# Layer 1's sum over neighbours of 24 batches computed in the second pass, beside the LSTM, and kept in DRAM

## The chip, the cores and the metric

The kernel runs on one core of a Trainium2 chip. The metric is the device time of one execution in microseconds (us). A core has five engines that run side by side, each with its own in-order queue of instructions: TensorE (PE; the loading of its weights is listed apart as PEld), VectorE (DVE), ScalarE (ACT), GpSimd (POOL) and SyncE (SP), which here issues nearly all of the DMAs.

## The reference

The input is x, 32 batches of 512 nodes with 128 features, and adj, a symmetric 0/1 matrix of 512x512 for each batch with ones on its diagonal. Four layers are applied, each to the ReLU of a normalised x, and each result is added to x. Layer 0 is attention masked by adj. Layer 1 is the one that the change touches:

```python
def preprocess_adj(A):
    A_hat = A + jnp.eye(N, dtype=A.dtype)
    d = jnp.sum(A_hat, axis=2)
    ...
    return d_inv[:, :, None] * A_hat * d_inv[:, None, :]      # d_inv = d ** -0.5

def gcn_dynamic_forward(x, A_norm, conv_w, conv_b, w_ih, w_hh, b_ih, b_hh):
    df_in = x[:, x.shape[1] - HID:, :]                         # the last 128 nodes
    dyn = jax.lax.conv_general_dilated(df_in, conv_w, ...) + conv_b[None, :, None]
    lw = lstm(dyn, w_ih, w_hh, b_ih, b_hh)                     # 128 steps, all batches at once
    agg = jnp.matmul(A_norm, x)
    return jax.nn.sigmoid(jnp.matmul(agg, lw))
```

The LSTM needs only the last 128 nodes of layer 0's result, and its output lw is needed only in the last product. So agg, the sum over neighbours, does not depend on the LSTM. Layer 2 has four message-passing steps, each with a sum over neighbours by the normalised matrix, and layer 3 one more.

## The kernel before

The kernel doesn't write its instructions down in their final order. It records operations with their engine, an estimated duration, a rank (lower is more urgent) and the tiles that they read and write; a planner, `Plan.run`, then plays them through with these durations and fixes each engine's order. A tile has a tag, and `BUFS` says how many buffers a tag has; an operation whose tile has no free buffer has to wait. On the chip each engine works through its list in that order, and an instruction that waits holds up all that is behind it on its queue.

There are three stages.

- **`pass_1(b)`** for all 32 batches: normalise x, project keys, queries and values, and compute attention for the last 128 nodes only, then the convolution. It keeps keys and hidden rows (`f_dkq`), values (`f_dv`) and the last 128 rows of x (`f_dl`) in DRAM.
- **`lstm()`** with **`pass_2(b)`** beside it. The 128 LSTM steps are urgent (rank below 1000). A step is: 16 small matmuls on PE (`f_z`, L1193), a tanh on ACT (L1219, and L1234 for the fourth gate), three operations on DVE that make the cell state (L1226 to L1228), a tanh on ACT (L1236), and two operations on DVE that write the hidden state (L1240, L1241); the next step's matmuls wait for it. Between them the planner puts `pass_2`, the attention of the other 384 nodes: load `f_kq`, three quarters of the rows of the matrix (`f_a`, 768 KB), `f_v` and x; then `f_pq` (L1259), four products `f_s` (L1268), exponentials and masks (L1271, L1272), twelve products `f_po` (L1277), the update of x (L1283) and its store `f_dx` (L1285), mean and variance (L1008, L1010), and the reciprocal root on POOL. `fold(i)` prepares layer 2's weights in the same stage. A filler that would run past the expected start of an urgent operation by more than 0.05 us is held back.
- **`rest(b)`**, the third stage, after the LSTM: load the whole matrix (1024 KB) and x, square the matrix on ACT (L1329; its accumulated rows are the degrees), make the degree factors on POOL (`norms`, L1335), normalise x with them (`ln_apply`), split the ReLU into two parts of a shorter number format (`relu_parts`, L1303 and L1304), add the identity to the matrix on DVE (L1356), sum over neighbours on PE (`aggregate`, L1313, eight matmuls of 128x512 into `f_pg`), take the identity off again, evict the sum (`f_gT`), and multiply it by the LSTM's output (`gates`, L1372). Then come layers 2 and 3. The matrix also goes to DRAM as bfloat16 (`f_das`, L1387, issued by POOL), comes back transposed (`f_aT`, L1389), and DVE compares the two (`f_junk`, L1392); if some matrix were not symmetric, a general kernel would run instead.

The batches of a stage overlap. The last two batches' `pass_2` is planned among the first batches of the third stage, and the first batches of `rest` begin before the LSTM has ended.

Of the kernel before, what the change touches and what calls it, by code (L numbers as in the profile page):

```python
# [520 lines left out]
class Plan:  # L521
# [19 lines left out]
    def __init__(self, bufs, fifo, banks):  # L541
        self.banks = banks
        self.last = float("inf")
        self.spared = float("inf")
        self.left = 0
        self.sealed = 0
        self.ops = []
        self.bufs = bufs
        self.made = {}
        self.fifo = {t: [] for t in fifo}  # L550
# [40 lines left out]
    def run(self, tc, queues):  # L591
# [63 lines left out]
        def room(o):  # L655

            at = 0.0
            need = {}
            for c in o.cells:
                if c not in seen:  # L660
                    if c.tag in self.fifo and self.fifo[c.tag][turn[c.tag] + need.get(c.tag, 0)] is not c:
                        return None
                    need[c.tag] = need.get(c.tag, 0) + 1
            for t, n in need.items():
                if len(slots[t]) < n + (t == self.banks and o.rank >= self.spared and self.left > 0):
                    return None
                at = max(at, sorted(slots[t])[n - 1])
            return at
# [4 lines left out]
        done, order = 0, []  # L673
        while done < len(ops):
            best = None
            for e, cands in pools.items():
                first = None
                held = expected.get(e)
                for rank, no, o in cands:
                    r = room(o)  # L680
                    if r is None:
                        continue
                    if r:
                        r += self.HOP
                    s = max(free[e], o.ready[e], r)
                    if len(o.engines) > 1:
                        mine = s + o.engines[e][0]
                        if any(max(free[x], o.ready[x], r) + o.engines[x][0] < mine - 1e-9 for x in o.engines if x != e):
                            continue
                    if rank < self.URGENT:  # L690
                        held = s
                    elif held is not None and s < held < s + o.engines[e][0] - 0.05:
                        continue
                    if first is None or s < first[0] - 1e-9:
                        first = (s, o)
                        if s <= free[e] + 1e-9:
                            break
                if first is not None and (best is None or first[0] < best[0]):
                    best = (first[0], e, first[1])
# [25 lines left out]
            order.append(o)  # L725
            done += 1
# [7 lines left out]
def symmetric(ctx, tc, x, adj, weights, cols, rows, lstm_b, prelu_a, out, fail):  # L734
# [19 lines left out]
    LATE = 2  # L754
    FOLDS = (4, 7, 10, 13)
    MOVED = range(2, B - 2)
    TURN = 32
    T_STEP, T_SWITCH = 0.26, 0.1
    assert D == P and N == 512

    BUFS = {"a": 2, "ar": 6, "x": 7, "xn": 5, "y": 5, "gs": 5, "inv": 4, "n0": 4, "n1": 4, "n2": 4, "n3": 4, "low": 3, "hp": 2, "dt": 2, "mm": 8, "st": 4, "mv": 4, "rs": 4, "sh": 4, "dg": 4, "dv": 4,
# [23 lines left out]
    def new(tag, shape, name, dtype=FP):  # L785
        return plan.cell(sb, tag, shape, dtype, name)
# [22 lines left out]
    def PE(rank, t, fn, r=(), w=(), **k):  # L809
        return plan.op({"PE": (t, fn)}, rank, r, w, **k)  # L810
# [209 lines left out]
    def ln_apply(rank, xc, mean, rstd, shift, r, name, relu=False):  # L1020

        xn = new("xn", (P, NT, P), f"f_xn_{name}")
# [224 lines left out]
    def pass_2(b):  # L1247
        R = 20_000 + b * 10 if b < B - LATE else 30_000 + (b - B + LATE) * 10 + 15
        dkq, dv, dl, dx = kept[b]
        a = new("ar", (P, NT, NR), f"f_a_{b}")  # L1250
        kq = new("y", (P, N + NR), f"f_kq2_{b}")
        v = new("n3", (P, NT, P + 1), f"f_v2_{b}")
        xc = new("x", (P, L, P), f"f_x2_{b}")
        DMA(R, 448, lambda: nc.sync.dma_start(kq.t, dkq.t), [dkq], [kq])
        DMA(R, 768, lambda: nc.sync.dma_start(a.t, adj[b, :, :NR].rearrange("(t p) j -> p t j", p=P)), [], [a])
        DMA(R, 258, lambda: nc.sync.dma_start(v.t, dv.t), [dv], [v])
        DMA(R, 192, lambda: nc.sync.dma_start(xc.t, x[b, :NR].rearrange("(t p) d -> p t d", p=P)), [], [xc])
        pq = bank(f"f_pq_{b}", (P, NR), whole=False)
        PE(R, t_mm(NR), lambda: nc.tensor.matmul(pq.t, w[:, W_Q, :], kq.t[:, N:], start=True, stop=True), [kq], [pq])  # L1259
# [6 lines left out]
        for j in range(NT):  # L1266
            s = bank(f"f_s_{b}_{j}", (P, NR), whole=False)
            PE(R, t_mm(NR), lambda s=s, j=j: nc.tensor.matmul(s.t, kq.t[:, bass.ts(j, P)], q.t, start=True, stop=True),  # L1268
               [kq, q], [s])
            e = new(f"n{j}" if j < 3 else "gs", (P, NR), f"f_e_{b}_{j}")  # L1270
            ACT(R, t_act(NR), lambda s=s, e=e: nc.scalar.activation(e.t, s.t, AF.Exp), [s], [e])  # L1271
            DVE(R, t_dve(NR), lambda e=e, j=j: nc.vector.tensor_mul(e.t, e.t, a.t[:, j, :]), [a], [e])  # L1272
            es.append(e)
# [11 lines left out]
        DMA(R + 5, 192, lambda: nc.sync.dma_start(dx.t, xc.t), [xc], [dx])  # L1285
# [3 lines left out]
        ln_rstd(R, mv, 0, L, (lambda: ln1[:, b, 1, :L], (l1, "rr")))  # L1289

# [17 lines left out]
    def aggregate(rank, parts, ar, pg):  # L1308

        for k in range(2):  # L1310
# [7 lines left out]
    def rest(b, lw_after):  # L1318
# [3 lines left out]
        ar = new("ar", (P, NT, N), f"f_ar_{b}", FR)  # L1322
# [4 lines left out]
        deg = new("dg", (P, NT), f"f_deg_{b}")  # L1327
        for t in range(NT):
            ACT(R, 0.62, lambda t=t: nc.scalar.activation(ar.t[:, t, :], a.t[:, t, :], AF.Square,  # L1329
                                                          accum_out=deg.t[:, t : t + 1]), [a], [(ar, t), (deg, t)])  # L1330
        dinv = new("dv", (P, TURN // NT, NT), f"f_dinv_{b}")
        l1 = lns[b]
        rs = new("rs", (P, NT), f"f_rs_c{b}")

        def norms():  # L1335
# [6 lines left out]
            nc.gpsimd.tensor_mul(rs.t, ln1[:, b, 1, :], d[:, 0, :])  # L1342
        POOL(R, 3.4, norms, [deg, l1], [dinv, rs])
        sh = new("sh", (P, NT), f"f_sh_c{b}")
        ln_shift(R, lambda: ln1[:, b, 0, :], rs, sh, [l1])
        xs = ln_apply(R, xc, lambda t: ln1[:, b, 0, t : t + 1], lambda t: rs.t[:, t : t + 1], lambda t: sh.t[:, t : t + 1],
                      [l1, rs, sh], f"c{b}")
        xp = relu_parts(R, xs, f"c{b}")
# [3 lines left out]
        pg = bank(f"f_pg_{b}")  # L1352

        def diagonal(op):
            blocks = flat(ar.t).rearrange("p (k c) -> p k c", c=P)[:, :: NT + 1, :]
            nc.vector.tensor_tensor(blocks, f32(blocks), ident.unsqueeze(1).to_broadcast([P, NT, P]), op)  # L1356

        DVE(R, t_dve(N), lambda: diagonal(OP.add), [], [ar])

        first = aggregate(R, xp, ar, pg)  # L1360
        DVE(R, t_dve(N), lambda: diagonal(OP.subtract), [], [ar])
        gT = new("gs", (P, N), f"f_gT_{b}")
        evict(R, N, lambda: gT.t, lambda: pg.t, [pg], [gT])
        plw = bank(f"f_plw_{b}", (P, P), whole=False)
        PE(R, T_TR, lambda: nc.tensor.transpose(plw.t, seq[:, :, b], ident), [], [plw], after=lw_after + [first])
# [94 lines left out]
        g3 = new("gs", (P, N), f"f_gT3_{b}")  # L1460
# [144 lines left out]
```

## Time and profile before

| | |
|---|---|
| median of 5 runs | 1339.12 us (1336.26 to 1342.03) |
| the profiled execution | 1338.86 us |
| its span, first to last instruction | 1337.1 us, granted TensorE clock 0.985 |
| busy share of the span | PE 96%, PEld 74%, DVE 76%, ACT 58%, POOL 27% |
| first LSTM matmul, last LSTM matmul group | 186.4 us, 498.5 us |
| moved by DMA | 215.99 MB, mean 162 GB/s |

The groups that the text speaks of (line, engine, operation, out<-in, shape, count, then busy us and mean ns of one, then the idle time of the engine before them):

```profile
L1313 PE MATMUL f_pg<-f_ar,f_xp_c 128*128 128x512 f32 x256 | 74.6, 417 | 4.2 <-ACT f_xp_c L1303 4.2
L1329 ACT ACTIVATE f_ar<-f_a 128x512 fp32r<-128x512 f32 x128 | 78.9, 621 | 3.5 <-PE f_pg L1313 2.1
L1028 ACT ACTIVATE f_xn_c<-f_x,f_sh_c,f_rs_c 128x128 f32<-128x128 f32 x199 | 86.7, 495 | 7.8 <-DVE f_sh_c L1036 7.6
```

Matmuls are pipelined and the ends of their spans are modelled, so the 417 ns of one are not its cost: the distance to the next start is.

### The profile page before, as it was taken

The numbers are of one execution on the slowest core, as the hardware profiler recorded it, in microseconds if no ns is written. First come the engines' busy times: TensorE is split into PE (matmuls) and PEld (weight loads), VectorE is DVE, ScalarE is ACT, GpSimd is POOL, SyncE is SP. The second block draws the span as 40 slices with busy tenths as digits, with TensorE's granted clock in tenths as the row PEclk, the third lists the DMA queues.
The fourth block names the chain that finished last, engine by engine and source line by source line (L and its number), as shares of the span: only waits on it lengthen the run. The fifth ranks groups of instructions, "written<-read, shape, count | busy, mean of one in ns | idle before, by whom it ended". The sixth has DMA issues, their size and how long they took to land. (4 is left out here: it accounts for less than half of the span.)

```text
span 1337.1 us, 26043 instructions
## 1 busy us (share of the span) xinstructions
PE 1286.6 (96%) x8830; PEld 993.4 (74%) x8830; DVE 1012.4 (76%) x3416; ACT 779.9 (58%) x1921; POOL 366.0 (27%) x689
## 2 busy tenths in 40 slices
PE   8999999999999938999999999999999999999996
PEld 6888877776666716787887887787787787787774
DVE  7888867777787848568787787787787787787645
ACT  5566645555556536556666666666666666665433
POOL 4654421111112213222332232232242232232101
PEclk9999999999999968999999999999999999999998
DMA  7879898976676366345566666566666566684211
GB/s 236 283 248 289 264 304 276 285 254 211 189 234 187 84 123 127 86 102 138 130 134 140 134 135 139 135 135 140 133 135 136 141 134 138 139 162 84 48 32 35
DMA packets 287199, 215.99 MB, mean 162 GB/s; under 512 B 136656, under 2 KB 249552, under 8 KB 287056
## 3 DMA queue, kind: packets, MB, share of 16 engines
q1 hardware_dynamic: 270160, 197.45, 54.0%
q0 software_dynamic: 16896, 16.78, 8.0%
q8 instruction: 72, 1.18, 0.4%
q14 instruction: 71, 0.58, 0.2%
HBM read 125.97 MB, written 56.75 MB: 137 GB/s over the span
## 5 line engine op out<-in xcount | busy, mean ns | idle before, releaser
L1313 PE MATMUL f_pa<-f_ar,f_y 128*128 128x512 f32 x1024 | 305.2, 430 | 0.0
L1313 PEld LDWEIGHTS f_pa<-f_ar,f_y 128*128 128x128 f32 x1024 | 189.1, 188 | 74.3 <-issue 41.4
L1419 PE MATMUL f_py<-f_wf,f_n 128*128 128x128 f32 x1280 | 173.9, 275 | 0.0
L1434 ACT ACTIVATE f_n<-f_pa,f_bcol 128x512 f32<-128x512 f32 x128 | 88.4, 691 | 144.0 <-PE f_pa L1430 143.9
L1419 PEld LDWEIGHTS f_py<-f_wf,f_n 128*128 128x128 f32 x1280 | 165.0, 192 | 9.1 <-issue 1.4
L1430 PE MATMUL f_pa<-f_n,f_wf 128*128 128x512 f32 x320 | 152.6, 592 | 0.0
L1387 POOL DMA_DIRECT2D f_das<-f_ar x32 | 37.0, 1155 | 371.5 <-DVE f_ar L1356 364.2
L1295 ACT CAST f_y<-f_py 128x512 fp32r<-128x512 f32 x128 | 74.5, 582 | 74.2 <-PE f_py L1419 50.0
L1277 PEld LDWEIGHTS f_po<-f_v,f_e 128*128 128x128 f32 x768 | 97.3, 191 | 22.8 <-issue 11.9
L1277 PE MATMUL f_po<-f_v,f_e 128*128 128x129 f32 x768 | 109.8, 283 | 0.0
L1193 PE MATMUL f_z<-f_w,f_seq 128*32 128x128 f32 x2040 | 84.1, 283 | 22.6 <-DVE f_seq L1241 16.9
L1426 DVE TENSOR_TENSOR f_pa<-f_pa,f_inv 128x512 f32<-128x512 f32 x128 | 88.3, 692 | 20.1 <-PE f_pa L1313 20.1
L1268 PE MATMUL f_s<-f_q,f_kq 128*128 128x384 f32 x256 | 101.2, 505 | 0.0
L1296 DVE TENSOR_TENSOR f_y<-f_py,f_y 128x512 fp32r<-128x512 f32 x128 | 86.9, 680 | 16.1 <-ACT f_y L1295 16.1
L1193 PEld LDWEIGHTS f_z<-f_w,f_seq 128*32 128x32 f32 x2040 | 49.3, 110 | 61.1 <-issue 15.7
L1392 DVE SCALAR_TENSOR_TENSOR f_junk<-f_a,f_aT 128x1024 bf16<-128x1024 f32 x64 | 78.2, 1222 | 19.6 <-DMA f_aT<-f_das 18.4
L1430 PEld LDWEIGHTS f_pa<-f_n,f_wf 128*128 128x128 f32 x320 | 57.8, 190 | 46.5 <-issue 38.1
L1028 ACT ACTIVATE f_xn_c<-f_x,f_sh_c,f_rs_c 128x128 f32<-128x128 f32 x199 | 86.7, 495 | 7.8 <-DVE f_sh_c L1036 7.6
L1329 ACT ACTIVATE f_ar<-f_a 128x512 fp32r<-128x512 f32 x128 | 78.9, 621 | 3.5 <-PE f_pg L1313 2.1
L840 DVE COPY f_gT<-f_pg 128x512 f32<-128x512 f32 x28 | 19.4, 691 | 79.9 <-PE f_pg L1313 79.8
L1313 PE MATMUL f_pg<-f_ar,f_xp_c 128*128 128x512 f32 x256 | 74.6, 417 | 4.2 <-ACT f_xp_c L1303 4.2
L1219 ACT ACTIVATE f_th<-f_z 128x96 f32<-128x96 f32 x128 | 32.0, 250 | 77.2 <-PE f_z L1193 75.4
(193 smaller groups left out, 2775.6 us busy)
## 6 DMA issues: line engine op xcount, KB each, us to landing
f_a<-in_adj_dram SPq DMA_DIRECT2D x32, 1024.0 KB
f_a<-in_adj_dram SPq DMA_DIRECT2D x32, 768.0 KB
f_das<-f_ar POOLq DMA_DIRECT2D x32, 512.0 KB, 5.1
f_dkq<-f_kh SPq DMA_DIRECT2D x32, 448.0 KB
f_kq<-f_dkq SPq DMA_DIRECT2D x32, 448.0 KB
f_dv<-f_v SPq DMA_DIRECT2D x32, 258.0 KB
f_v<-f_dv SPq DMA_DIRECT2D x32, 258.0 KB
f_x<-in_x_dram SPq DMA_DIRECT2D x32, 256.0 KB
```

The source lines that it names most:

```text
L1028: nc.scalar.activation(xn.t[:, t, :], xc.t[:, t, :], AF.Relu, bias=shift(t), scale=rstd(t))
L1193: nc.tensor.matmul(z.t[part, k, :, :], h, w[:, m : m + 4, part], start=False, stop=True, skip_group_check=True)
L1268: PE(R, t_mm(NR), lambda s=s, j=j: nc.tensor.matmul(s.t, kq.t[:, bass.ts(j, P)], q.t, start=True, stop=True), [kq, q], [s])
L1277: PE(R, t_mm(P), lambda t=t, j=j: nc.tensor.matmul(po.t[:, t, :], es[j].t[:, bass.ts(t, P)], v.t[:, j, :], start=(j == 0), stop=(j == NT - ...
L1296: DVE(rank, t_dve(N), lambda: nc.vector.tensor_sub(parts.t[:, :, 1, :], src.t, f32(parts.t[:, :, 0, :])), [src, (parts, 0)], [(parts, 1)])
L1313: nc.tensor.matmul(pg.t, parts.t[:, j, k, :], ar.t[:, j, :], start=(k == 0 and j == 0), stop=(k == 1 and j == NT - 1))
L1329: ACT(R, 0.62, lambda t=t: nc.scalar.activation(ar.t[:, t, :], a.t[:, t, :], AF.Square, accum_out=deg.t[:, t : t + 1]), [a], [(ar, t), (de ...
L1392: nc.vector.scalar_tensor_tensor(junk, flat(a.t[:, 2 * k : 2 * k + 2, :]), 1.0, flat(aT.t[:, 2 * k : 2 * k + 2, :]), OP.mult, OP.not_equal ...
L1419: nc.tensor.matmul(py.t[:, j, :], nodes[n].t[:, bass.ts(j, P)], wf[:, W_F[i] + c, 0, :], start=False, stop=(c == nch - 1), skip_group_chec ...
L1426: before = DVE(R, t_dve(N), lambda pa=pa: nc.vector.tensor_mul(pa.t, pa.t, inv_row.t), [inv_row], [pa])
L1430: nc.tensor.matmul(pa.t, wf[:, W_F[i] + c, 1, :], nodes[n].t, start=False, stop=(c == nch - 1), skip_group_check=True)
L1434: ACT(R, 0.57, lambda pa=pa, n=n, i=i: nc.scalar.activation(n.t, pa.t, AF.Tanh, bias=bcol[:, i : i + 1]), [pa], [n])
```

## The change

For the batches 0 to 23 (`EARLY`), `pass_2` now also computes layer 1's sum over neighbours. It loads the whole matrix into a buffer of tag `a` and squares it on ACT into tag `ar`; the attention's mask is read from that. It loads the last 128 rows of x too. After the reciprocal root it makes the degree factor on POOL, normalises x in place, splits it, adds the identity to the matrix (on POOL for these batches), sums over neighbours with eight matmuls that are now eight separate operations for the planner, evicts the sum into the tile of x, and stores it in DRAM (`f_dgT`, 256 KB). `rest` loads it from there (`f_gT3`) and has no identity to add and to take off for these batches; it still squares the matrix and makes the degree factors. The batches 24 to 31 are computed as before.

For all batches, keys and hidden rows are loaded as two tiles instead of one, and some tags and counts of buffers change. In the planner, a filler may now run past the expected start of an urgent operation by 0.15 us instead of 0.05, the LSTM step's matmuls are planned with 0.24 us instead of 0.26, and the last free bank of PSUM isn't given to an operation that is ranked far behind the most urgent one left.

```diff
@@ Plan.run @@
+                if len(slots[t]) == n and t in self.kept and by_rank and o.rank > by_rank[-1].rank + 12:
+                    return None
...
-                    elif held is not None and s < held < s + o.engines[e][0] - 0.05:
+                    elif held is not None and s < held < s + o.engines[e][0] - 0.15:
@@ symmetric @@
+    EARLY = range(24)
-    T_STEP, T_SWITCH = 0.26, 0.1
+    T_STEP, T_SWITCH = 0.24, 0.1
...
@@ pass_2 @@
-        a = new("ar", (P, NT, NR), f"f_a_{b}")
-        kq = new("y", (P, N + NR), f"f_kq2_{b}")
+        early = b in EARLY
+        a = new("a" if early else "ar", (P, NT, N if early else NR), f"f_a_{b}")
+        keys = new("inv", (P, N), f"f_k2_{b}")
+        hT = new("xn", (P, NR), f"f_h2_{b}")
...
+        if early:
+            DMA(R, 1024, lambda: nc.sync.dma_start(a.t, adj[b].rearrange("(t p) j -> p t j", p=P)), [], [a])
+            ar, deg = squares(R, b, a, "2")
+            mask, rows_of = ar, lambda j: f32(ar.t[:, j, :NR])
...
+        if early:
+            d = new("dg", (P, NT), f"f_d2_{b}")
+
+            def root():
+                nc.gpsimd.tensor_scalar_add(d.t, deg.t, 1.0)
+                nc.gpsimd.tensor_tensor(d.t, d.t, neg_half[:, 0, :], OP.pow)
+            POOL(R, 1.3, root, [deg], [d])
+            rs = new("rs", (P, NT), f"f_rs_2{b}")
+            POOL(R, 0.34, lambda: nc.gpsimd.tensor_mul(rs.t, ln1[:, b, 1, :], d.t), [d, l1], [rs])
+            gT, _ = sums_of_1(R, b, xc, ar, rs)
+            dg = plan.fixed(dram.tile([P, N], FP, tag=f"g{b}", name=f"f_dgT_{b}"))
+            DMA(R + 5, 256, lambda: nc.sync.dma_start(dg.t, flat(gT.t)), [gT], [dg])
+            kept_sums[b] = dg
+    def diagonal(rank, ar, op, either=False):
+        def on(engine):
+            def fn():
+                blocks = flat(ar.t).rearrange("p (k c) -> p k c", c=P)[:, :: NT + 1, :]
+                engine.tensor_tensor(blocks, f32(blocks), ident.unsqueeze(1).to_broadcast([P, NT, P]), op)
+            return fn
+        if either:
+            POOL(rank, 1.4, on(nc.gpsimd), [], [ar])
+        else:
+            DVE(rank, t_dve(N), on(nc.vector), [], [ar])
+    def sums_of_1(rank, b, xc, ar, rs):
+        l1 = lns[b]
+        sh = new("sh", (P, NT), f"f_sh_c{b}")
+        ln_shift(rank, lambda: ln1[:, b, 0, :], rs, sh, [l1])
+        xs = ln_apply(rank, xc, lambda t: ln1[:, b, 0, t : t + 1], lambda t: rs.t[:, t : t + 1], lambda t: sh.t[:, t : t + 1],
+                      [l1, rs, sh], f"c{b}", place=xc if b in EARLY else None)
+        xp = relu_parts(rank, xs, f"c{b}")
+        pg = bank(f"f_pg_{b}")
+        diagonal(rank, ar, OP.add, b in EARLY)
+        first = aggregate(rank, xp, ar, pg, b in EARLY)
+        gT = xc if b in EARLY else new("gs", (P, N), f"f_gT_{b}")
+        evict(rank, N, lambda: gT.t if b not in EARLY else flat(gT.t), lambda: pg.t, [pg], [gT])
+        return gT, first
@@ rest @@
+        if b in EARLY:
+            gT, first = new("inv", (P, N), f"f_gT3_{b}"), None
+            DMA(R, 256, lambda: nc.sync.dma_start(gT.t, kept_sums[b].t), [kept_sums[b]], [gT])
+        else:
+            gT, first = sums_of_1(R, b, xc, ar, rs)
+            diagonal(R, ar, OP.subtract)
```

## The prediction

> **What bounds the kernel now.** First the windows, one stage to a line (stretch in us: its length, busy us of PE, PEld, DVE, ACT and POOL with row counts, granted clock, DMA share, GB/s). The LSTM runs from 186 to 501 with the second pass beside it, the third stage from there on.
>
> ```profile
> 186.00:260.00 74.00, 73.66 (x817) 52.10 (x815) 54.64 (x265) 39.55 (x142) 11.75 (x24) 1.00 0.91 286
> ...
> 330.00:440.00 110.00, 109.24 (x1152) 73.19 (x1148) 86.63 (x413) 62.55 (x226) 21.08 (x44) 1.00 0.66 200
> 440.00:475.00 35.00, 32.99 (x358) 22.16 (x358) 26.75 (x132) 18.43 (x68) 11.05 (x19) 1.00 0.42 90
> 475.00:501.00 26.00, 5.50 (x81) 2.68 (x81) 11.79 (x48) 7.08 (x31) 3.09 (x6) 0.53 0.56 125
> 501.00:520.00 19.00, 14.46 (x64) 11.90 (x65) 13.54 (x54) 13.00 (x36) 8.38 (x13) 0.74 0.46 84
> ...
> 600.00:1200.00 600.00, 600.00 (x3215) 471.99 (x3214) 475.62 (x1219) 387.33 (x863) 172.26 (x261) 1.00 0.63 137
> ```
>
> PE is the candidate everywhere but in 475 to 501, where it has 5.5 us of work in 26. A busy PE is a modelled number, so I went to the PE timeline for what really passes (start, length, what):
>
> ```profile
> 434.84 0.64 PE L1193 MATMUL f_z<-f_w,f_seq 128*32 128x128 f32 x16
> 435.42 2.05 PE L1277 MATMUL f_po<-f_v,f_e 128*128 128x129 f32 x16
> 437.40 0.64 PE L1193 MATMUL f_z<-f_w,f_seq 128*32 128x128 f32 x16
> 437.97 0.71 PE L1277 MATMUL f_po<-f_v,f_e 128*128 128x129 f32 x4
> 438.52 1.46 PE L1268 MATMUL f_s<-f_q,f_kq 128*128 128x384 f32 x4
> 439.91 0.64 PE L1193 MATMUL f_z<-f_w,f_seq 128*32 128x128 f32 x16
> ```
>
> An LSTM step is the distance between two f_z groups: 2.56 and 2.51 us. What stands between them, the filler, costs 16 x 0.112 = 1.79 us in the first step, 4 x 0.112 + 4 x 0.323 = 1.74 in the second (start-to-start medians of those rows over 200 to 440; an fp32 matmul leaves two rows). Both times the step is filler + 0.77. I laid the instruction order beside the trace for the first 119 steps: fillers of 1.52, 1.57, 1.63 and 1.74 go with 2.29, 2.33, 2.39 and 2.51 us, and below 1.4 the step stays at 2.14 to 2.28, the recurrence's own latency. The rule gives 284.9 us for the 119; they took 284.6 (186.4 to 471.0). So PE sets the pace of the LSTM stage, and there is no room in it except in the last eight steps, which have no filler and took 27.5 us. The timeline shows why they took so long:
>
> ```profile
> 481.89 1.74 SPq L1389 DMA_TRANSPOSE f_aT<-f_das  x1
> 481.95 1.23 DVE L1392 SCALAR_TENSOR_TENSOR f_junk<-f_a,f_aT 128x1024 bf16<-128x1024 f32 x1 [6.76 <-DMA f_aT<-f_das]
> ```
>
> The symmetry check waits 6.76 us on DVE's queue for a transposed matrix, the LSTM's cell update stands behind it (one step of about 10 us), and PE then runs at a clock of 0.53.
>
> In the third stage the PE timeline has the sum over neighbours (f_pg) back to back with everything else:
>
> ```profile
> 812.84 1.09 PE L1313 MATMUL f_pg<-f_ar,f_xp_d 128*128 128x512 f32 x4
> 813.77 1.07 PE L1313 MATMUL f_pg<-f_ar,f_xp_c 128*128 128x512 f32 x4
> 814.68 1.07 PE L1313 MATMUL f_pa<-f_ar,f_y 128*128 128x512 f32 x4
> ```
>
> Four of them take 0.91 us to the next group, 0.228 each. PE bounds this stage; DVE has 79% and ACT 65%.
>
> **The change, part by part.** The instruction order of the changed kernel shows how much moves. Of layer 1's 256 matmuls (f_pg from f_xp_c), 16 stood inside the LSTM and 240 behind it; now 192 and 64. So 176 move, at 0.228: 40.1 us. Seventeen second-pass matmuls go from before or within the LSTM to behind it (12 f_po at 0.224, one f_pq and four f_s at 0.646): 5.9 us.
>
> Third stage: -41 (40.1 by the median; 42.2 by the group's mean spacing of 0.240 in 600 to 1200), +5.9. What goes with the matmuls (two diagonals of 0.68, a ReLU split of 0.68, normalisation and eviction, on DVE and ACT) was hidden behind PE and gives nothing. New is a 256 KB load of the kept sum for each of 24 batches; some 23 us of PE work per batch cover it at a DMA share of 0.63. The start of the stage loses filler: there the chain of the first batch is bare, and sums of later batches filled it. I price this, and stalls further on, at +5. Bounds: 0 (the clock, 0.74 in 501 to 520, should now stay full) and 15 (the 4.5 us idle in that line three times over).
>
> LSTM stage: fillers summed over the new order are 226 us between 128 steps (before 189; 40.1 more, 3.2 less for five matmuls gone). With filler + 0.77 and a floor of 2.2 the 127 gaps come to 325 us, against 312.1 (186.4 to 498.5). That is +12.9, not +37, because the eight empty steps and their stall are filled.
>
> Other engines here. ACT gets four squares of 0.61 per early batch, a ReLU of 0.63, LN tiles of 0.49 and evictions of 0.60: its filler in the stage goes from 96 to 171 us. DVE's goes from 119 to 153. Gap by gap between the LSTM's own instructions (about 0.67 us free on ACT before the second tanh, step - 1.1 after it), 11 steps exceed the PE time, by 2 us in all: +2. POOL gets the diagonal, which no row shows: 457 ns for a 128x128 tensor_tensor (L942) and 212 for 128x4 (L1342) give an estimate of 1.2 us for 512 columns. With the roots (0.25 + 1.05 on 4 columns) that is 60 us on an engine with 16% in the stage, hidden; uncovered it would delay each sum by 1.2, 29 us in all.
>
> DMA. An early batch took 448 + 768 + 258 + 192 + 192 = 1858 KB, now 2434: 13.8 MB more, 48 us at 286 GB/s if bare. A batch now lasts about 11 us, which asks for 226 GB/s, so the stage's other work covers it. SP's queue issues 124 more DMAs of about 0.35 us, 43 us, on a queue that waits most of the time. Ahead of the LSTM the last neighbour load of pass 1 stands behind 1.45 MB more, 5 us at 286 GB/s; on the other side 11 f_po (2.5 us) leave that stretch, in which PE is the busiest. I take 0, bounds -2.5 and +5.
>
> New waits. The normalisation now overwrites the tile that f_dx is being stored from, so it must wait for that store; behind it on ACT's and DVE's queues stand the tanh and cell update of the LSTM, and behind those PE. In the new order two to three steps lie between the last write of the tile and this instruction, 4.5 to 7 us. The trace's landing records of f_dx say 1.9 to 6.1 us from issue, median 3.5, plus about 0.6 to the issue. Half of the batches have nothing to spare, and a step of 2.55 has 0.4 over the recurrence's 2.14. Bounds: 0, and 24 x 2.1 = 50 (all landing at 6.1). I take +4, near 0, since the first 119 steps now show under 2 us that the rule doesn't explain, though two early sums are among them. The symmetry check still stands in the last steps, but its transpose has 8.5 steps (21.7 us) from the cast instead of 13.5 us; the last one needed 20.2. I take +2 of 0 to 9.5.
>
> Sum: 12.9 + 2 + 4 + 2 - 41 + 5.9 + 5 = -9.2. The profiled execution took 1338.86 us around a span of 1337.1; the median of the five runs is 1339.12. So 1327.9 for the span, 1330 for the median.
>
> **The rivals.**
> (1) The stored tile is late, slower. If landings stretch towards 6.1 us under the fuller DMA, half of the batches lose 2.1 us: 25 instead of 4, 1351. It decides from 17 us, 0.7 per batch; above that the kernel is slower. For it: share 0.91 in 186 to 260, and in-order queues. Against it: DMA waits of PE in 200 to 450 are 0.5 us in all.
> (2) The third stage doesn't shrink by its PE time. Its f_pa rows already sit 0.270 apart instead of 0.230, 30 us in 24 batches, waiting for ACT and DVE. With less filler half of the 41 may turn into such gaps: 1350. Against it: two or three batches interleave, and ACT and DVE lose work too.
> (3) The LSTM stage has room. PEld is busy 73 of 110 us in 330 to 440, and 37 idle us there alone would nearly hold the 40 moved. Then the stage stays at 312: -41 + 5.9 + 5, 1309. Against it stands the step rule above. The Trainium skill (Perfetto Trace Analysis, section Identifying the Most-Contended Engine) takes weight-load busy time, not matmul busy time, as the measure of TensorE headroom; by that rule this rival would hold, and this trace's steps speak against it.
> (4) POOL blocks DVE. 24 diagonals of 1.2 us that stop the cell update, less 0.4 of slack, cost 19 us: 1349. Against it: DVE's f_e products under a running POOL power take 544 ns, others 542. The Trainium skill (SBUF — State Buffer, section SBUF: two separate sides) has GpSimd and two-input VectorE instructions lock one shared port pair for a whole instruction; for the power rows the trace doesn't agree.
>
> **How the numbers follow.** Forecast 0.55, own range 1320 to 1340; (1) 0.21, (2) 0.13, (3) 0.06, (4) 0.05. Low end: clean, with the larger saving, 12.9 - 42.2 + 5.9 - 2.5 = -26, 1313. High end: (1) and a little, 1354. About 0.3% (4 us) is what a measurement can tell. Faster by more: 0.47 of the forecast and (3), 0.53. Within: 0.08 of the forecast and 0.08 of (1), (2) and (4) at a smaller size, 0.16. Slower: 0.31.
>
> **What would show it.** f_z groups should run 128 steps in some 333 us with a mean step near 2.6; longer steps with the same filler, ended by f_dx or by POOL, are (1) or (4). From the last f_z to the end should be near 808 us (now 838.6), and a batch of the third stage near 23.2 us (25.0 now); 24 or more is (2). A stage that stays at 312 is (3). An LSTM that starts after 191 makes the sum wrong in a place I took for 0.

## The result, and the profile after

The changed kernel takes 1335.75 us (median of 33 runs, 1331.35 to 1340.73), the kernel before 1338.5 beside it (58 runs): ratio 0.9979, 95% interval 0.9972 to 0.9986. It is faster, by 2.8 us where the prediction had 9. The profiled span went from 1337.1 to 1334.5 us.

Three distances in the traces of the profiled executions hold the whole difference: start of the program to the first f_z group, first to last of the 128 f_z groups (the LSTM stage), and last f_z group to the end (the rest).

| | LSTM starts | LSTM stage | rest | span |
|---|---|---|---|---|
| before | 186.4 | 312.1 | 838.6 | 1337.1 |
| predicted | 186.4 | 333 | 808.5 | 1327.9 |
| after | 182.9 | 344.1 | 807.5 | 1334.5 |

The rest came as predicted. The stage was 11 us longer than predicted and took back most of it; an earlier start gave 3.5. The windows after, in the same columns as those of before (stretch; length, then busy us of PE, PEld, DVE, ACT and POOL with row counts; granted clock, DMA share, GB/s):

```profile
330.00:440.00 110.00, 104.78 (x1059) 72.61 (x1058) 93.00 (x389) 75.38 (x267) 40.10 (x62) 1.00 0.70 219
...
475.00:501.00 26.00, 25.92 (x278) 17.75 (x276) 20.41 (x94) 15.60 (x56) 6.51 (x12) 1.00 0.89 250
...
520.00:560.00 40.00, 30.80 (x172) 22.04 (x171) 28.69 (x111) 24.45 (x80) 18.97 (x33) 0.87 0.90 203
600.00:1200.00 600.00, 600.00 (x3259) 471.17 (x3259) 441.71 (x1151) 393.71 (x846) 168.49 (x258) 1.00 0.65 146
```

The hole at 475 to 501 is filled (PE 25.9 us of 26, clock 1.00). A smaller one opened at 520 to 560, where PE idles 9.2 us behind the LSTM. From 330 to 440 PE was busy 109.2 of 110 us before and is busy 104.8 now, with more filler to run: something new stops it. POOL doubled there, 21 to 40 us. The PE groups that moved, within the LSTM stage and behind it (count, then busy us and mean ns):

```profile
L1380 PE MATMUL f_pg<-f_ar,f_xp_c 128*128 128x512 f32 x192 | 57.0, 422 | 0.3 <-DVE f_xp_c L1373 0.2
```

```profile
L1386 PE MATMUL f_pg<-f_ar,f_xp_c 128*128 128x512 f32 x64 | 19.0, 424 | 0.6 <-ACT f_xp_c L1372 0.6
```

192 and 64, as the instruction order had said. PE's timeline in the third stage shows one transpose f_plw for each batch:

```profile
784.93 0.27 PE L1424 MATMUL f_plw<-f_ident,f_seq 128*128 128x128 f32 x1
...
808.32 0.27 PE L1424 MATMUL f_plw<-f_ident,f_seq 128*128 128x128 f32 x1
```

A batch whose sum was kept takes 23.4 us. Batches that still make theirs stand 25.2 apart, in this kernel as in the one before (the prediction had 25.0).

**Where the stage is long.** The rule of the prediction (a step is its filler plus 0.77, at least 2.2) gives 325.2 us with the fillers of the new trace, and the stage took 344.1. The 18.9 us between are no drift. They sit in some 25 single steps, about one for each early batch, 0.2 to 1.7 us each. One of them, the step from 329.13 to 332.50, in the timeline (start, length, engine, line, operation; idle before it in brackets):

```profile
328.62 0.98 DVE L1291 TENSOR_TENSOR f_e<-f_e,f_ar 128x384 f32<-128x384 f32 x2
328.68 1.19 POOL L1024 TENSOR_TENSOR f_ln<-f_ln,f_neg_half 128x3 f32<-128x3 f32 x1
...
329.13 0.64 PE L1200 MATMUL f_z<-f_w,f_seq 128*32 128x128 f32 x16
...
329.70 2.05 PE L1296 MATMUL f_po<-f_v,f_e 128*128 128x129 f32 x16
...
329.85 1.27 POOL L1338 TENSOR_TENSOR f_ar<-f_ar,f_ident 128x512 fp32r<-128x512 f32 x1
329.90 1.26 DVE L1233 SCALAR_TENSOR_TENSOR f_cu<-f_th,f_c 128x32 f32<-128x32 f32 x1 [0.30 <-ACT f_th L1226]
331.07 0.20 POOL L1317 TENSOR_TENSOR f_rs<-f_ln,f_d 128x4 f32<-128x4 f32 x1
331.09 0.23 DVE L1234 SCALAR_TENSOR_TENSOR f_cv<-f_th 128x32 f32<-128x32 f32 x1
...
332.50 0.65 PE L1200 MATMUL f_z<-f_w,f_seq 128*32 128x128 f32 x16 [0.75 <-DVE f_sh_c L1043]
```

DVE's first operation of the cell update (L1233) works on 32 columns and takes 0.19 us as a rule. Here it begins 0.05 us behind POOL's diagonal (L1338) and takes 1.26: it ends when POOL does. All that follows is late by that much, and PE, done with its filler at 331.75, waits. The line of the step's end names f_sh_c, the DVE instruction last before it; the cause stands five rows higher. The two rows on top show the contrast: under POOL's power (L1024, three columns, also two operands) DVE's two products f_e take 0.98 us together, their usual time.

The group of the first cell operation, then POOL's diagonal, 23 of the 24 of which lie in the stage (min/median/max ns):

```profile
L1233 DVE SCALAR_TENSOR_TENSOR f_cu<-f_th,f_c x126: 157/192/1300, 188.0 to 525.4; 128x32 f32<-128x32 f32 x126
```

```profile
L1338 POOL TENSOR_TENSOR f_ar<-f_ar,f_ident x23: 1258/1276/1612, 184.6 to 464.7; 128x512 fp32r<-128x512 f32 x23
```

Counted over the stage, 23 DVE rows of several lines are longer than their group's median by more than 0.1 us, 22.3 us together. Every one lies under an L1338 row of POOL, none under another. That is rival (4) of the prediction, to which it gave 0.05. The trace suggests it; the experiments had to show it.

### The profile page after: what moved, and what is told of

Read it like the earlier page. It is cut to its first block, busy times and chain, and to the rows that moved or that the text cites. A ratio compares the mean times of both kernels' runs of the same rounds, so it can differ in the third digit from the quotient of the medians.

```text
span 1334.5 us, 26489 instructions
## 1 busy us (share of the span) xinstructions
PE 1289.7 (97%) x8832; PEld 991.0 (74%) x8832; DVE 1009.3 (76%) x3388; ACT 833.3 (62%) x2093; POOL 421.1 (32%) x761
## 5 line engine op out<-in xcount | busy, mean ns | idle before, releaser
L1386 PE MATMUL f_pa<-f_ar,f_y 128*128 128x512 f32 x1024 | 301.3, 431 | 0.2 <-ACT f_y L1364 0.2
L1330 ACT ACTIVATE f_ar<-f_a 128x512 fp32r<-128x512 f32 x224 | 138.7, 621 | 9.6 <-DMA f_a<-in_adj_dram 7.5
L1446 POOL DMA_DIRECT2D f_das<-f_ar x32 | 27.9, 872 | 344.8 <-ACT f_ar L1330 273.7
L1287 PE MATMUL f_s<-f_q,f_k 128*128 128x384 f32 x256 | 100.6, 502 | 1.4 <-DMA f_k<-f_dkq 1.3
L1386 PE MATMUL f_pg<-f_ar,f_xp_d 128*128 128x512 f32 x256 | 73.8, 410 | 0.0
L1478 PE MATMUL f_py<-f_wf,f_T_c 128*128 128x128 f32 x448 | 73.0, 275 | 0.7 <-ACT f_py L929 0.7
L1290 ACT ACTIVATE f_e<-f_s 128x384 f32<-128x384 f32 x128 | 61.9, 487 | 16.3 <-PE f_s L1287 15.3
L1063 DVE COPY f_hl_d<-f_n 128x1024 uint16<-128x1024 uint16 x25 | 17.3, 694 | 66.6 <-ACT f_n L1493 66.6
```

What stands on the lines that cost most here:

```text
L1287: PE(R, t_mm(NR), lambda s=s, j=j: nc.tensor.matmul(s.t, keys.t[:, bass.ts(j, P)], q.t, start=True, stop=True), [keys, q], [s])
L1330: ACT(rank, 0.62, lambda t=t: nc.scalar.activation(ar.t[:, t, :], a.t[:, t, :], AF.Square, accum_out=deg.t[:, t : t + 1]), [a], [(ar, t), ...
L1386: nc.tensor.matmul(pg.t, parts.t[:, j, k, :], ar.t[:, j, :], start=(k == 0 and j == 0), stop=(k == 1 and j == NT - 1))
L1478: nc.tensor.matmul(py.t[:, j, :], nodes[n].t[:, bass.ts(j, P)], wf[:, W_F[i] + c, 0, :], start=False, stop=(c == nch - 1), skip_group_chec ...
```

## The experiments

The planner makes a new order whenever a cost, a tile or an engine changes, on all engines at once. That is so in the first group of runs and in the last run told. In the others only what a planned operation issues was exchanged, with the cost that the planner counts left alone: their order on PE, ACT and SP is the changed kernel's, instruction for instruction, and on DVE and POOL only the rows in question differ.

### With a new order

**The diagonal on DVE.**

```diff
-        diagonal(rank, ar, OP.add, b in EARLY)
+        diagonal(rank, ar, OP.add)
```

> The changed kernel with one thing undone: the identity is added to the squared matrix on DVE (0.68 us an operation) instead of POOL (1.27 us); all 24 early sums stay where they are. Theory P (POOL's 512-column operation with two operands from SBUF stops DVE's operations with two operands, and the LSTM's cell update with them): the lengthened DVE rows (0.19 us become 1.26 to 1.32) vanish, the LSTM stage falls from 344 us to 326 to 332, the total from 1336 to 1318 to 1325. Rival L (the stage is long because stores and loads land late in fuller queues, the in-place normalisation above all): the stage stays at 340 to 346, the total at 1334 to 1338. Rival D (DVE has no room for 24 x 0.68 = 16 us beside the LSTM): stage 338 to 346, but its long steps end on DVE rows of ordinary length.

Measured: 1422.16 us, ratio to before 1.0612 (1.0594 to 1.063), a miss. The lengthened rows are gone, but the stage is 337.2 us where theory P had 326 to 332, 11.0 over its own rule of 326.2 instead of 18.9. And the rest took 900.3 us. Its windows behind the LSTM:

```profile
560.00:600.00 40.00, 28.38 (x89) 19.71 (x90) 12.47 (x30) 6.92 (x15) 5.57 (x9) 0.66 0.41 104
600.00:700.00 100.00, 65.84 (x261) 43.09 (x259) 27.54 (x77) 30.07 (x64) 11.50 (x20) 0.88 0.24 52
```

PE idles a third of this stretch, with DVE and ACT under a third busy: in the timeline one batch's steps follow each other with a wait between each two, and no second batch fills the gaps. This is the new order and not DVE's load, as a later run shows; why the planner chose it stays open. One of the stage's long steps (416.13 - 411.72 = 4.41 us) is what the prediction called rival (1), the stored tile that is late:

```profile
414.00 0.86 DVE L1032 TENSOR_SCALAR f_x<-f_x,f_ln,f_rs 128x128 f32<-128x128 f32 x3 [2.12 <-DMA f_dx<-f_x]
414.78 0.18 DVE L1233 SCALAR_TENSOR_TENSOR f_cu<-f_th,f_c 128x32 f32<-128x32 f32 x1
```

The in-place normalisation waits 2.12 us for the store, and the cell update stands behind it. So that mechanism exists, here and there. The run decides nothing on the total.

**The normalised tile apart from the stored one.**

```diff
-                      [l1, rs, sh], f"c{b}", place=xc if b in EARLY else None)
+                      [l1, rs, sh], f"c{b}")
```

> The changed kernel, but the early normalisation writes a tile of its own instead of overwriting the one that f_dx is stored from, so it need not wait for that store; the diagonal stays on POOL. Rival L as the prediction had it (the stored tile is late): the stage loses 4 to 19 us, total 1317 to 1332. Theory P: no change beyond what a new order of the instructions brings, stage 341 to 347, total 1333 to 1339; the 20-odd DVE rows under a POOL diagonal stay long.

Measured: 1339.87 us, 1.0009 (1.0 to 1.0018). The stage is 340.9, the rest 814.4 in its new order; stage and total lie just outside what theory P had. Without any wait for f_dx the stage stays 14.5 us over its rule (326.4), and 20 DVE rows under the diagonals are still lengthened, 19.8 us in all. Rival (1) is not what makes it long.

**POOL's diagonal in four.**

```diff
-            POOL(rank, 1.4, on(nc.gpsimd), [], [ar])
+            for t in range(NT):
+                def fn(t=t):
+                    block = ar.t[:, t, t * P : (t + 1) * P]
+                    nc.gpsimd.tensor_tensor(block, f32(block), ident, op)
+                POOL(rank, 0.46, fn, [], [ar])
```

> The changed kernel with POOL's diagonal in four operations of 128 columns (about 0.46 us each) instead of one of 512 columns. Theory P with a stop that lasts as long as one POOL instruction: a DVE operation is held for at most 0.46 us at a time, of which a step's slack of about 0.4 hides the most; but the cell update is three such operations in a row and can be held three times: excess of the stage over the filler rule between 4 and 15 us (18.9 before), total 1322 to 1332. If the stop lasts as long as POOL has work in its queue, nothing changes: 1334 to 1338, with DVE rows of 1.3 us and more. Rival L: no change, and no DVE row over 0.4 us that should take 0.2.

Measured: 1343.59 us, 1.0044 (1.003 to 1.0058), a miss: the stage fell to 336.5 as expected (11.9 over its rule), but the rest grew to 821.0 with the new order.

**One operand on POOL.**

```diff
-        diagonal(rank, ar, OP.add, b in EARLY)
+        diagonal(rank, ar, OP.add)
+        if b in EARLY:
+            blocks = flat(ar.t).rearrange("p (k c) -> p k c", c=P)[:, :: NT + 1, :]
+            POOL(rank, 1.4, lambda: nc.gpsimd.tensor_scalar_mul(blocks, f32(blocks), 1.0), [], [ar])
```

> The diagonal on DVE as in the first of these runs, and on POOL in its old place an operation on the same 512 columns with one operand from SBUF (times 1.0, in place, about as long). If it is the second operand that stops DVE, the stage is that of the first run, 326 to 333, total 1318 to 1326. If any POOL operation that reads and writes 512 columns of SBUF stops DVE's two-operand operations, the DVE rows are lengthened again by about the length of the POOL operation, and the total is 1332 to 1340. Rival L makes nothing of it: as the first run, whatever that gave.

Measured: 1337.89 us, 0.9983 (0.9971 to 0.9994); stage 335.3, rest 817.9. DVE's short rows beside POOL's 1.56 us took 0.33 to 0.63: lengthened, but not for the length of the operation. The total falls into the range of the second reading, but by its rest and not by stops of that length: again it says more of the order than of the cause.

### With the order kept

| in the place of the 24 early diagonals | stage (profile) | rest (profile) | median us | ratio to before (95%) |
|---|---|---|---|---|
| POOL, one of 512 columns (the change) | 344.1 | 807.5 | 1335.75 | 0.9979 (0.9972 to 0.9986) |
| nothing | 329.9 | 807.2 | 1322.79 | 0.9883 (0.9864 to 0.9902) |
| POOL, three of 512 columns | 405.8 | 807.2 | 1399.18 | 1.0448 (1.0429 to 1.0467) |
| POOL, one operand, 512 columns | 332.6 | 804.1 | 1323.25 | 0.9890 (0.9873 to 0.9907) |
| POOL, four of 128 columns | 337.5 | 807.2 | 1328.82 | 0.9931 (0.9917 to 0.9945) |
| DVE, at POOL's places | 338.5 | 804.6 | 1328.03 | 0.9914 (0.9897 to 0.9931) |
| DVE, behind the LSTM's last operation | 330.0 | 806.2 | 1321.92 | 0.9881 (0.9864 to 0.9898) |

The filler rule gives 325.2 us for every line of it, since PE's order is the same.

**No diagonal.**

```diff
-            POOL(rank, 1.4, on(nc.gpsimd), [], [ar])
+            POOL(rank, 1.4, lambda: None, [], [ar])
```

> The changed kernel with its instruction order kept on every engine, but the 24 POOL operations that add the identity in the early sums left out (so layer 1's sums lack each node's own term in 24 batches). Theory P: 23 lengthened DVE rows vanish; what is left over the filler rule (325 us) is the stalls with another cause, about 1 us each in steps 0, 9, 48 and 124: the LSTM stage is 327 to 332 us instead of 344, the rest from the last step on stays at 808, the total falls from 1336 to 1318 to 1325. Rival L (late stores and loads of the fuller queues make the long steps): the stage stays at 340 to 345, the total at 1331 to 1337.

Measured: 1322.79 us. The stage fell by 14.2 us, the rest stayed within 0.3. The cell operation's group now has no long row:

```profile
L1233 DVE SCALAR_TENSOR_TENSOR f_cu<-f_th,f_c x127: 157/193/207, 188.3 to 515.0; 128x32 f32<-128x32 f32 x127
```

What is left over the rule is 4.7 us, mostly in steps 0 (0.8), 9 (1.1, the load of the weights that `fold` prepares for layer 2) and 124 (1.3). Rival L, at 340 to 345, is out.

**Three operations for one.**

```diff
-            POOL(rank, 1.4, on(nc.gpsimd), [], [ar])
+            def thrice():
+                for o in (OP.add, OP.subtract, OP.add):
+                    on(nc.gpsimd, o)()
+            POOL(rank, 1.4, thrice, [], [ar])
```

> The same order on every engine, but POOL adds the identity, takes it away and adds it again: three operations of 1.27 us in place of one, result the same. Theory P: DVE is stopped up to three times a batch, between 24 x 0.8 = 19 us (two more single stops) and 24 x 2.5 = 61 us more: stage 360 to 405, total 1353 to 1398. Rival L: only the sums start 2.5 us later, which costs under 5 us: total 1334 to 1341.

Measured: 1399.18 us, stage 405.8, both about 1 us over the top of what theory P allowed: 61.7 us for 48 more operations. The first of a batch costs 14.2 / 24 = 0.59, since a step's slack takes a part of the 22.3 us by which the DVE rows grew. One batch in the timeline:

```profile
408.40 4.60 POOL L1338 TENSOR_TENSOR f_ar<-f_ar,f_ident 128x512 fp32r<-128x512 f32 x3
...
408.83 1.24 DVE L1043 SCALAR_TENSOR_TENSOR f_sh_c<-f_ln,f_rs 128x4 f32<-128x4 f32 x1
...
410.46 1.25 DVE L1233 SCALAR_TENSOR_TENSOR f_cu<-f_th,f_c 128x32 f32<-128x32 f32 x1
411.63 0.18 DVE L1234 SCALAR_TENSOR_TENSOR f_cv<-f_th 128x32 f32<-128x32 f32 x1
411.84 1.20 DVE L1235 SCALAR_TENSOR_TENSOR f_c<-f_cu,f_cv 128x32 f32<-128x32 f32 x1
```

Each POOL operation here catches one DVE operation and holds it to its end; over the stage there are 67 lengthened DVE rows for 69 such operations. Between two of them DVE gets in what fits (0.55 us of f_e at 409.99, one of the cell's three), and the next is caught again. It goes the other way too: the first two additions of this row begin while DVE is at an f_e product, and they show 1.65 and 1.54 us where the third shows 1.26. Not all of the 61.7 us are stops. PE's pauses now reach 3 us, and after most of those over 1.9 us its clock falls for a step:

```profile
204.50:207.30 2.80, 0.43 (x2) 0.00 (x0) 2.77 (x5) 1.46 (x5) 2.60 (x3) 1.00 1.03 374
207.40:211.70 4.30, 4.30 (x30) 3.58 (x30) 2.06 (x8) 1.55 (x5) 1.18 (x1) 0.62 0.18 62
```

The second window is one step at a clock of 0.62, in which PE never waits: 4.38 us where its filler asks for 2.80. Thirteen such steps are 20 us over the rule. That leaves 41 us of stops, 0.86 for each added operation.

**One operand.**

```diff
-            POOL(rank, 1.4, on(nc.gpsimd), [], [ar])
+            def one():
+                blocks = flat(ar.t).rearrange("p (k c) -> p k c", c=P)[:, :: NT + 1, :]
+                nc.gpsimd.tensor_scalar_mul(blocks, f32(blocks), 1.0)
+            POOL(rank, 1.4, one, [], [ar])
```

> The same order on every engine; in the diagonal's place POOL multiplies the same 512 columns by 1.0 in place, one operand from SBUF instead of two (the identity is not added in 24 batches). In an earlier run this operation took 1.56 us and beside it DVE's rows of 0.19 us took 0.33 to 0.63, not 1.26 to 1.32. If a two-operand POOL operation is what stops DVE: the total is that of the run without diagonals, plus at most 4 us. If any POOL operation that reads SBUF stops DVE for its whole length: as the changed kernel, 1333 to 1340, with DVE rows of 1.5 us. From the earlier rows I expect something between, 1320 to 1330.

Measured: 1323.25 us, as without diagonals, although POOL is busy longer (1.58 us each). The longest first cell operation is 0.63 us:

```profile
L1233 DVE SCALAR_TENSOR_TENSOR f_cu<-f_th,f_c x127: 157/192/627, 187.5 to 516.5; 128x32 f32<-128x32 f32 x127
```

32 DVE rows are lengthened, 10.3 us in all, 0.3 each, and the slack of a step hides most of that (the stage is 2.7 us over the run without diagonals). So POOL being busy on the same columns of SBUF is not what cost the time; it takes the addition of two tensors. The two operations differ in their kind as well as in the number of operands, and no run here separates these.

**Four of 128 columns.** 

> The changed kernel's order on every engine, POOL's diagonal issued as four operations of 128 columns (0.51 us each in the earlier run) in the place of the one. If POOL stops DVE for the length of one instruction, each stop is shorter, but the cell update's three operations can be caught one after the other: stage between that without diagonals and that with one operation, 333 to 340 us (329.9 and 344.1), total 1325 to 1333. If DVE is kept out as long as POOL's queue has such work, nothing changes: 1334 to 1338, with DVE rows of 1 us and more.

```diff
-            POOL(rank, 1.4, on(nc.gpsimd), [], [ar])
+            POOL(rank, 1.4, four, [], [ar])
```

(`four` issues the four operations of the earlier edit.) Measured: 1328.82 us, half way, with 72 rows longer than in the run without diagonals, by 0.2 us each, 16.2 in all. The group of the first cell operation:

```profile
L1233 DVE SCALAR_TENSOR_TENSOR f_cu<-f_th,f_c x127: 156/193/490, 187.2 to 520.8; 128x32 f32<-128x32 f32 x127
```

The stop ends with the instruction (0.51 us on the mean), but the cell's three operations can be caught in a row, as expected (0.49, 0.49 and 0.38 us behind 447.9). Against the same edit with a new order (1343.59) the stage differs by 1.0 us, the rest by 13.8.

**DVE at POOL's places.**

```diff
-            POOL(rank, 1.4, on(nc.gpsimd), [], [ar])
+            POOL(rank, 1.4, on(nc.vector), [], [ar])
```

> The same order on PE, ACT and SP, with the 24 diagonals issued on DVE at the place in time where POOL had them. Theory P: each costs DVE 0.68 us, of which the step's slack of about 0.4 takes a part: 24 x 0.3 = 7 us at most over the run without diagonals; stage 328 to 338, total 1320 to 1331. The first of the earlier runs, whose order was made anew, went to 1422 with 900 us behind the LSTM; if that came of the order and not of DVE's load, this one has 806 to 812 us there.

Measured: 1328.03 us; the rest is 804.6, so the 900 of the first run was its order. The stage is 8.6 us over the run with no diagonal, a little more than the bound of 7. It is not 24 equal parts. In step 77 DVE first waits for a store and then has the diagonal to do, with the cell update behind both (2.0 us over the rule):

```profile
390.23 0.35 DVE L1032 TENSOR_SCALAR f_x<-f_x,f_ln,f_rs 128x128 f32<-128x128 f32 x1 [1.68 <-DMA f_dx<-f_x]
390.49 0.69 DVE L1338 TENSOR_TENSOR f_ar<-f_ar,f_ident 128x512 fp32r<-128x512 f32 x1
...
391.34 0.18 DVE L1233 SCALAR_TENSOR_TENSOR f_cu<-f_th,f_c 128x32 f32<-128x32 f32 x1
```

PE pauses for 1.94 us, and step 78, with nothing to wait for, takes 1.6 more than its filler asks for, at a clock of 0.56 (window 392.80 to 396.70). The same happens in steps 124 and 125, where ACT waits for a matrix: 2.1 and 1.2. No diagonal stands near these two, and the run with one operand lost 1.8 and 1.4 there, so not all of the 8.6 us are the diagonal's. The profiled execution was also the slowest of six (1331.58 us); by the medians the run is 5.2 us over the one without diagonals.

**DVE behind the LSTM's last operation.** The diagonal is put on a list, and the next LSTM step issues it behind its transpose; f_pg issues it where none came before.

```diff
                 nc.vector.transpose(seq[:, t, :], h.t)
+                if waiting:
+                    waiting.pop(0)[1]()
...
-            POOL(rank, 1.4, on(nc.gpsimd), [], [ar])
+            POOL(rank, 1.4, lambda: waiting.append((ar, on(nc.vector))), [], [ar])
```

> The same order on PE, ACT, POOL and SP; each of the 24 diagonals is issued on DVE directly behind the next LSTM step's last DVE operation, when PE has a group of f_z and ACT a tanh to do before DVE's next cell update. If DVE's 0.68 us cost something in the run that put them at POOL's places because they stood ahead of a cell update, they cost less here: stage 330 to 335, total 1321 to 1327. If it is DVE's load as such, this run is like that one: stage 335 to 340, total 1326 to 1331.

Measured: 1321.92 us, stage 330.0: the sum's full result at the price of none, 1.2% under the kernel before and 1.0% under the change (0.9881 / 0.9979). The same step as in the first timeline, with its successor (lines are three higher in this kernel):

```profile
322.47 0.64 PE L1201 MATMUL f_z<-f_w,f_seq 128*32 128x128 f32 x16
...
323.04 2.05 PE L1299 MATMUL f_po<-f_v,f_e 128*128 128x129 f32 x16
...
323.24 0.19 DVE L1234 SCALAR_TENSOR_TENSOR f_cu<-f_th,f_c 128x32 f32<-128x32 f32 x1 [0.30 <-ACT f_th L1227]
...
324.37 0.21 DVE L1249 STREAM_TRANSPOSE f_seq<-f_h 128x32 f32<-128x32 f32 x1
324.50 0.65 DVE L1341 TENSOR_TENSOR f_ar<-f_ar,f_ident 128x512 fp32r<-128x512 f32 x1
325.02 0.64 PE L1201 MATMUL f_z<-f_w,f_seq 128*32 128x128 f32 x16
```

The step takes 2.55 us instead of 3.37. The diagonal runs while DVE has nothing of the LSTM to do: PE must first finish its f_po (325.09), run f_z, and ACT its tanh. So DVE's load as such costs nothing. Against this run the one before is 6.1 us longer in the medians, and 0.0033 (4.4 us) by the ratios to the kernel before, taken beside each; how much of that is the place ahead of the cell update alone, and how much the late store that it waits behind in a step like 77, one profile of each doesn't tell.

### With a new order again

**The planner's settings alone.**

```diff
-    EARLY = range(24)
+    EARLY = range(0)
```

> The changed kernel with no early sums at all (an empty set of batches): only the planner's new settings and the separate loads of keys and transposed features are left of the change. If the move is what changes the time, this is the kernel before: stage 308 to 316 us, the rest 832 to 842, total 1333 to 1343, and an LSTM start of 184 to 188. If the settings bring the gain of the third stage (807 us behind the LSTM instead of 839), the rest is below 825 here too.

Measured: 1342.59 us, 1.0039 (1.0025 to 1.0053): the settings by themselves cost time. The rest (833.9) is nearly that of before, so the third stage's gain is the sums'. The stage was a miss: 326.6 where I expected 308 to 316. The new settings put more of the second pass into the early steps (the rule gives 317.4), and 7.2 us more are in the last 16 steps, which have hardly any filler again, at a clock of 0.62 (466 to 510 us). The sums fill these. The prediction set a rule (325) against a measured time (312.1) and put the 12.9 us down to the sums. Rule against rule it is 302.5 before (284.9 for 119 steps, 2.2 for each of the last eight), 317.4 with the settings and 325.2 with the sums: most of it belongs to the settings. Measured, the stage with the sums and without their diagonals is 3.3 us longer than with the settings alone (329.9 and 326.6), though in another order.

## Why the prediction was right in its sign and wrong in its size

By its own terms, in spans:

| term | predicted | measured | by |
|---|---|---|---|
| LSTM start | 0 | -3.5 | 186.4 to 182.9 |
| stage, filler rule | +12.9 | +13.1 | the rule with the new trace's fillers: 325.2 - 312.1 |
| ACT and DVE overrun, stored tile, symmetry check | +8 | +4.7 | no diagonal: 329.9 - 325.2 |
| POOL's diagonal | 0 | +14.2 | 344.1 - 329.9 |
| third stage | -30.1 | -31.1 | 838.6 to 807.5 |
| sum | -9.2 | -2.6 | |

**The step that failed** is "POOL gets the diagonal [...] hidden". I took POOL's 16% for room and priced the diagonal's effect on DVE at nothing. The length was right (1.2 estimated, 1.28 measured) and so was the count. I even worked out what would happen if it blocked the cell update (24 x 0.8 = 19 us; the run without it says 14.2), and set it aside because of the power rows, beside which f_e took 544 ns and not 542. That observation still holds. But a power on 3 to 8 columns is no stand-in for an addition on 512: its two-operand form is the same, but its columns are some hundredth; that this is what spares DVE is not shown. The Trainium skill's rule (SBUF — State Buffer, section SBUF: two separate sides: whichever of GpSimd's and DVE's two-operand instructions starts first has the shared port pair to its end) spoke against this very part of the change. Here the trace agrees with it for POOL's addition on 512 columns, to the length (1.27 beside 1.26). It does not for the powers (no effect) nor for POOL's one-operand product on the same columns (0.3 us of 1.58), though both read SBUF.

**Right:** the filler rule: the fillers of the new trace give 325.2 where the prediction had 325, and with POOL's diagonals out of the way the 127 steps took 4.7 us more than that; that PE's matmuls leave the third stage for their full time (rival 2 predicted half; a batch fell from 25.2 to 23.4, predicted 25.0 to 23.2; the settings alone gave 4.7 of the 31.1 us); that the LSTM stage has no room (rival 3 falls: 329.9 even with no diagonal). **Smaller than allowed for:** the 8 us of lateness and stalls, measured 4.7. Rival (1) showed in single steps in several runs, up to 2.1 us of wait, never in half of the batches; but a wait that stops PE for 1.9 us costs nearly twice its length, by the clock, and the prediction's 25 us for it had no such term. **Not seen coming:** the start, 3.5 us earlier. The seven kernels of one order start between 182.4 and 186.6, so part of this may be scatter of that stretch; all twelve profiles with the new settings average 183.9, 2.5 earlier than the one profile of before, which is the lower bound that the prediction gave for the 11 f_po that leave it. Which it is stays open. Without it the measured terms add up to +0.9: that the sign came out right is luck as far as the sum goes. That the kernel is faster rests on the medians.

## What to carry to other kernels

An engine with room is no free place for an operation if that operation can stop the engine that holds the critical chain, as POOL's addition stopped DVE's cell update here. Take its price from a row of the same form and size, not of the same operation only, and ask for each operation of the chain what can hold it. When a planner remakes the order for every edit, exchange single operations with the order kept before believing any total: the same edit differed by 15 and by 94 us in its two orders here, more than the effect that was looked for.

## What the runs showed that was not expected

- Two POOL operations on the same 512 columns and about as long differ in what they do to DVE: with two operands DVE's rows of 0.19 us became up to 1.32 in the changed kernel, with one at most 0.64. A power of two operands on 3 or 4 columns, 1.0 to 1.2 us long, did nothing to it.
- PE's clock falls after short pauses. In the run with three POOL operations 12 of the LSTM stage's 16 pauses of 1.9 to 3.3 us were followed by a step at 0.5 to 0.6 of the clock, some 1.6 us long in excess; no pause of 1.81 us or less in that stage was, in any of the seven kernels of one order. What spared the other four seems to be where they lie in time. In that stage the granted clock falls for 3.41 us, once for 6.83, at times that are whole multiples of 3.41 us apart. Over the 3.41 us ahead of each of the twelve falls PE was busy 0.17 to 0.44 of the time. Cut at the same times, no stretch around the four spared pauses has less than 0.43; the longest pause of all, 3.25 us, lies across two stretches (0.48 and 0.57). The Trainium skill (TensorE: Matmul & The Clock Gate, section Part 1: The HAM clock gate (the "warmup" mystery)) has the clock halved after an idle window of about 3.4 us; pauses of little more than half of that were enough here.
- A DVE operation that is stopped shows as a long row, not as idle time: DVE looked busier (93.0 us in 330 to 440 where 86.6 stood before, some 8.5 of them such lengthening), and in the LSTM stage only 1.5 us of DVE's waits name POOL, none of them its diagonal.
